# A 16-batch graph kernel: the first batch prepared in a fixed order, its adjacency loaded first on two queues, two layer norms in halves

## Chip, cores, metric

One core of a Trainium2 chip. The metric is the device time of one execution in microseconds (us), the median of several; the runs of any one kernel below lie within 0.24% of each other. A difference between two kernels counts as shown where the intervals of their ratios to the kernel before do not overlap; where they do, a trace must show it.

In the lines of profiles PE is TensorE, PEld its weight loads, DVE VectorE, ACT ScalarE, POOL GpSimd and SP the sync engine; a q behind a name is the part of an engine that issues DMAs. L12 is line 12 of the kernel that was run. One float32 matmul stands there as two records (x2): the 16 first products of a batch count as x32.

## What is computed

Two layers, each with a residual and a layer norm, over 16 graphs of 1024 nodes with 128 features. `adj` is 16 x 1024 x 1024 in float32, 4 MB a graph; `x` is 0.5 MB a graph.

```python
# layer 0
degree = adj.sum(axis=-1)[:, :, None]
agg = einsum('bid,bij->bjd', x, adj) / degree
x = layernorm(x + relu(concat([x, agg]) @ W.T + b))
# layer 1: four sublayers, the last two with the earlier features concatenated
def sub(nodes, ws, bs, wd, bd, wn, bn, wu, bu):
    src = einsum('bjv,bij->biv', nodes @ ws + bs, l2norm(adj, 2))   # rows scaled
    dst = einsum('bjv,bji->biv', nodes @ wd + bd, l2norm(adj, 1))   # columns scaled
    return tanh(concat([src, nodes @ wn + bn, dst]) @ wu + bu)
x = layernorm(x + sub(sub(...)))
```

## The kernel before

The four weights of a sublayer are folded once at the start: `ws`, `wd` and `wn` are each multiplied by their part of `wu`. The adjacency of a graph is then used in two forms: `a`, its columns scaled by `cinv`, and `at`, transposed, with its rows scaled by `rinv`. While TensorE multiplies one batch, the other engines prepare the next; only the first batch is prepared while TensorE has no matmuls of an earlier batch to run. This setup and first batch (the *head*) and the last norm (the *tail*) are what the change touches. Names that come up: `xn`, x with the nodes on the partitions; `pa`, the first products of x and the adjacency; `agT`, these divided by the degree; `pw`, their product with `W`; `pt` and `t`, the messages of a sublayer before and after their bias; `pd`, the aggregation of messages.

```python
with tc.tile_pool(name="setup", bufs=1) as sp:       # memory that later pools reuse
    make_identity(nc, ident)                          # GpSimd
    ...                                               # fold, mean, group: VectorE
    nc.scalar.dma_start(w0n, w0)
    for l, (ws, bs, wd, bd, wn, bn, wu, bu) in enumerate(layers):
        ...                                           # 8 loads a layer on ScalarE's queue
    for l, (wr, wur, bc) in enumerate(raw):           # folding: TensorE, copies on VectorE
        ...
        nc.vector.tensor_add(bo, pm[:, 2 * P:2 * P + 1], bc[:, 3:4])   # L139: bout

def load(b):                                          # all on one queue
    for h in range(NH):                               # two halves of the rows
        for g in range(G):                            # 4 groups of 32 partitions
            nc.sync.dma_start(a[g * C:(g + 1) * C, ks], av[g])
        for g in range(G):
            nc.sync.dma_start(xn[g * C:(g + 1) * C, ks], xv[g])   # L164
    ...

def sums(b, a, state, rows):
    for i in rows:
        nc.vector.reduce_sum(...)                     # degree
        nc.scalar.activation(sq, a[:, i, :], AF.Square, accum_out=...)
        nc.gpsimd.tensor_add(acc, acc, sq)            # L187, column sums, one after the other

# the first batch, in an order left to the scheduler
xn, xs, a = load(0)
sums(0, a, st, ALL); column_sums(0, st); inverses(0, st)
(cinv, dinv), rinv = inverse_rows(0, st, False)       # through a DRAM scratch
yT = first_gnn(0, xn, to_features(xs, "x0_", False), a, dinv)
ys, s = norm_begin(xs, yT, "0_0")
scale_columns(a, cinv, FIRST)
v = norm_centre(xs, ys, s, "0_0")
...
with tc.manual_schedule(engines={eng.PE, eng.DVE, eng.Activation}):
    for b in range(B):
        ...                                           # batch b, and batch b+1 prepared beside it
    ys, s = norm_begin(xs, f4, f"1_{B - 1}")          # the last norm, all 1024 nodes at once
    v = norm_centre(xs, ys, s, f"1_{B - 1}")
    rstd = norm_rstd(v, f"1_{B - 1}")                 # GpSimd power on 128x32
    norm_end(xs, rstd)
    store(B - 1, xs)
```

Of the kernel before, what the change touches and what calls it, by code (L numbers as in the profile page):

```python
# [23 lines left out]
def adj_resnorm_kernel(ctx: ExitStack, tc: tile.TileContext, x, adj, w0, b0, layers, out):  # L24
# [50 lines left out]

    fold = const.tile([P, P], F32, name="fold")
# [3 lines left out]
    nc.vector.memset(mhalf, -0.5)  # L80

    w0T = const.tile([P, 2, P], F32, name="w0T")
    b0c = const.tile([P, 1], F32, name="b0c")
    wall, bsd, bout = [], [], []

    with tc.tile_pool(name="setup", bufs=1) as sp:
        ident = sp.tile([P, P], F32, name="ident")
        make_identity(nc, ident)
        nc.vector.reduce_sum(fold[:, :C], ident.rearrange("p (g c) -> p c g", g=G), axis=AX.X)
        for g in range(1, G):  # L90
            nc.vector.tensor_copy(fold[:, g * C:(g + 1) * C], fold[:, :C])
        nc.vector.tensor_scalar_mul(mean, fold, 1.0 / D)
        nc.vector.reduce_sum(group, ident.rearrange("p (g c) -> p g c", g=G), axis=AX.X)
        w0n = sp.tile([P, 2 * P], F32, name="w0n")
        nc.scalar.dma_start(w0n, w0)
        nc.scalar.dma_start(b0c, b0.rearrange("(p o) -> p o", o=1))
        raw = []
        for l, (ws, bs, wd, bd, wn, bn, wu, bu) in enumerate(layers):
            nch = CHUNKS[l]
            wr = sp.tile([P, 3, nch, P], F32, name=f"wr{l}")  # L100
            for k, w in enumerate((ws, wd, wn)):
                nc.scalar.dma_start(wr[:, k], w.rearrange("(c p) v -> p c v", p=P))
            wur = sp.tile([P, 3, P], F32, name=f"wu{l}")
            nc.scalar.dma_start(wur, wu.rearrange("(c p) v -> p c v", p=P))
            bc = sp.tile([P, 4], F32, name=f"bc{l}")
            for k, v in enumerate((bs, bd, bn, bu)):
                nc.scalar.dma_start(bc[:, k:k + 1], v.rearrange("(p o) -> p o", o=1))
            raw.append((wr, wur, bc))

        pt = ps_t.tile([P, BPH, P], F32, tag="pt", name="w0tr")  # L110
        for k in range(2):
            nc.tensor.transpose(pt[:, k], w0n[:, k * P:(k + 1) * P], ident)
        nc.vector.tensor_copy(w0T, pt[:, :2])


        part = (0, 2, 1)
        for l, (wr, wur, bc) in enumerate(raw):
            nch = CHUNKS[l]
            wt = const.tile([P, nch, 3, P], F32, name=f"wall{l}")
            for c in range(nch):  # L120
                pt = ps_t.tile([P, BPH, P], F32, tag="pt", name=f"wtr{l}_{c}")
                for k in range(3):
                    nc.tensor.transpose(pt[:, k], wr[:, k, c], ident)
                wT = sp.tile([P, 3, P], F32, name=f"wT{l}_{c}", tag="wT", bufs=2)
                nc.vector.tensor_copy(wT, pt[:, :3])
                pm = ps_mm.tile([P, HW], F32, tag="mm", name=f"wm{l}_{c}")
                for k in range(3):
                    nc.tensor.matmul(pm[:, k * P:(k + 1) * P], wT[:, k], wur[:, part[k]],
                                     start=True, stop=True)
                nc.vector.tensor_copy(wt[:, c].rearrange("p k v -> p (k v)"), pm[:, :3 * P])  # L130
            pm = ps_mm.tile([P, HW], F32, tag="mm", name=f"bm{l}")
            for k in range(2):
                nc.tensor.matmul(pm[:, k * P:(k + 1) * P], bc[:, k:k + 1].to_broadcast([P, P]),
                                 wur[:, part[k]], start=True, stop=True)
            nc.tensor.matmul(pm[:, 2 * P:2 * P + 1], wur[:, part[2]], bc[:, 2:3], start=True, stop=True)
            bb = const.tile([P, 2 * P], F32, name=f"bsd{l}")
            nc.vector.tensor_copy(bb, pm[:, :2 * P])
            bo = const.tile([P, 1], F32, name=f"bout{l}")
            nc.vector.tensor_add(bo, pm[:, 2 * P:2 * P + 1], bc[:, 3:4])  # L139
            wall.append(wt)  # L140
            bsd.append(bb)
            bout.append(bo)
# [3 lines left out]
    stage = ctx.enter_context(tc.tile_pool(name="stage", bufs=3))  # L146

# [21 lines left out]
    def store(b, xs):  # L169
        ov = out[b].rearrange("(k r) (g f) -> g r k f", r=C, g=G)  # L170
        for g in range(G):
            nc.sync.dma_start(ov[g], xs[g * C:(g + 1) * C])

    def sums(b, a, state, rows):

        if not state:
            state["cols"] = two.tile([P, 3 * NB], F32, tag="cols", name=f"cols{b}")
            state["acc"] = one.tile([P, N], F32, tag="acc", name=f"acc{b}")
        cols, acc = state["cols"], state["acc"]
        for i in rows:  # L180
            nc.vector.reduce_sum(cols[:, 2 * NB + i:2 * NB + i + 1], a[:, i, :], axis=AX.X)  # L181
            sq = two.tile([P, N], F32, tag="sq", name=f"sq{b}_{i}")
            nc.scalar.activation(sq, a[:, i, :], AF.Square, accum_out=cols[:, i:i + 1])  # L183
            if i == 1:
                nc.gpsimd.tensor_add(acc, state["sq"], sq)
            elif i > 1:
                nc.gpsimd.tensor_add(acc, acc, sq)  # L187
            state["sq"] = sq
# [8 lines left out]

    def inverses(b, state):
# [10 lines left out]
        inv = two.tile([P, C], F32, tag="inv", name=f"inv{b}")  # L209
        nc.gpsimd.memset(inv[:, 3 * NB:], 0.0)  # L210
        nc.gpsimd.tensor_tensor(inv[:, :2 * NB], cols[:, :2 * NB], mhalf[:, :2 * NB], ALU.pow)
        state["inv"] = inv

    def inverse_rows(b, state, scaled):


        cols, inv = state["cols"], state["inv"]
        if scaled:
            nc.vector.tensor_mul(cols[:, 2 * NB:], cols[:, 2 * NB:], inv[:, NB:2 * NB])
        nc.vector.reciprocal(inv[:, 2 * NB:3 * NB], cols[:, 2 * NB:])  # L220
        tr = two.tile([P, C], F32, tag="invt", name=f"invt{b}")
        nc.vector.transpose(tr, inv)
        dr = scratch.tile([P, C], F32, tag="dr", name=f"dr{b}")
        nc.sync.dma_start(dr, tr)
# [7 lines left out]
        nc.vector.tensor_copy(rinv, pr)  # L232
        rows = []
# [7 lines left out]
        return rows, rinv  # L241

    def scale_columns(a, cinv, rows):
        for i in rows:
            nc.vector.tensor_mul(a[:, i, :], a[:, i, :], cinv)  # L245
# [12 lines left out]
    def norm_begin(xs, fT, name):  # L258
        ys = one.tile([P, K, C], F32, tag="acc", name=f"y{name}")
        nc.vector.transpose(ys.rearrange("p k f -> p (k f)"), fT)  # L260
        nc.vector.tensor_add(ys, ys, xs)
        s = two.tile([P, K], F32, tag="part", name=f"s{name}")
        nc.vector.reduce_sum(s, ys, axis=AX.X)
        return ys, s

    def norm_centre(xs, ys, s, name):
        pm = small(f"pm{name}")
        nc.tensor.matmul(pm, mean, s, start=True, stop=True)
        nc.vector.tensor_sub(xs, ys, pm[:, :, None].to_broadcast([P, K, C]))
        sq = two.tile([P, K, C], F32, tag="sq", name=f"sq{name}")  # L270
        nc.scalar.activation(sq, xs, AF.Square)
        v = two.tile([P, K], F32, tag="part", name=f"v{name}")
# [3 lines left out]
    def norm_rstd(v, name):  # L276
        pv = small(f"pv{name}")
        nc.tensor.matmul(pv, mean, v, start=True, stop=True)  # L278
        ve = two.tile([P, K], F32, tag="ve", name=f"ve{name}")
        nc.vector.tensor_scalar_add(ve, pv, LN_EPS)  # L280
        rstd = two.tile([P, K], F32, tag="rstd", name=f"rs{name}")
        nc.gpsimd.tensor_tensor(rstd, ve, mhalf, ALU.pow)  # L282
        return rstd

    def norm_end(xs, rstd):
        nc.vector.tensor_mul(xs, xs, rstd[:, :, None].to_broadcast([P, K, C]))  # L286
# [79 lines left out]


    FIRST, LAST, ALL = range(BPH), range(BPH, NB), range(NB)
    xn, xs, a = load(0)
    st = {}  # L370
    sums(0, a, st, ALL)
    column_sums(0, st)
    inverses(0, st)
    (cinv, dinv), rinv = inverse_rows(0, st, False)
    yT = first_gnn(0, xn, to_features(xs, "x0_", False), a, dinv)
    ys, s = norm_begin(xs, yT, "0_0")
    scale_columns(a, cinv, FIRST)
    v = norm_centre(xs, ys, s, "0_0")
    scale_columns(a, cinv, LAST)
    at = transposed(0)  # L380
    rows = [load_rows(0, q) for q in range(3)]
    scale_rows(rows[0], 0, rinv)
    rstd = norm_rstd(v, "0_0")
    transpose_rows(rows[0], 0, at)
    norm_end(xs, rstd)
    x1T = to_features(xs, "x1_0_", True)
    rows.append(load_rows(0, 3))
    for q in range(1, NQ):
        scale_rows(rows[q], q, rinv)
        transpose_rows(rows[q], q, at)  # L390
# [3 lines left out]
    eng = mybir.EngineType  # L394
    late = None
    with tc.manual_schedule(engines={eng.PE, eng.DVE, eng.Activation}):
# [133 lines left out]
```

## Time and profile before

| | before |
|---|---|
| median of 3 runs | 2744.63 us (2743.38 to 2747.24) |
| span of the profiled run | 2742.0 us |
| head: start to the first aggregation matmul | 109.2 us |
| block: from there to the end of the last matmul | 2610.4 us |
| tail: from there to the end | 22.4 us |

The three parts are read off the timeline and add up to the span. TensorE's busy share of 97% therefore does not close the matter: the block is nearly all TensorE and stays, and the other 132 us are open to change. The profile lines are shown in the prediction below.

### The profile page before, as it was taken

The page shows a single profiled execution, that of the slowest core. Times are in us where ns is not written, and L with a number is a line of the kernel's source. Part 1 is how long each engine was busy: PE and PEld are TensorE (multiplying, and loading weights), DVE is VectorE, ACT ScalarE, POOL GpSimd, SP SyncE. Part 2 cuts the span into 40 slices and gives each one's busy share as a digit, 9 for nine tenths or more (in the row PEclk, how much of TensorE's full clock was granted, in tenths as well). Part 3 has the DMA queues.
Part 4 walks back from the last instruction along what each step waited for, and adds up shares of the span by engine and source line. Part 5 has one row for each costly group of instructions (what it writes and reads, how often), then busy time and mean ns, then how long its engine had stood idle before and what let it go on. Part 6 is the DMA issues. An engine that isn't in the chain of part 4 may idle for free.

```text
span 2742.0 us, 18638 instructions
## 1 busy us (share of the span) xinstructions
PE 2661.1 (97%) x7257; PEld 1365.0 (50%) x7257; DVE 1150.7 (42%) x1581; ACT 286.9 (10%) x449; POOL 515.2 (19%) x182
## 2 busy tenths in 40 slices
PE   5699999999999999999999999999999999999996
PEld 3255554455545455554455545455554455545453
DVE  3634436253352634436253352634436253452501
ACT  1010101001010010101001010010101001010000
POOL 2021303113130121303113130121303113030100
PEclk8799999999999999999999999999999999999998
DMA  6811516134061431516134061431516134061100
GB/s 117 174 35 37 97 35 122 32 80 81 19 116 35 84 70 37 98 35 120 34 78 83 18 117 35 83 71 37 98 35 119 35 78 83 18 119 27 22 2 8
DMA packets 352504, 179.98 MB, mean 66 GB/s; under 512 B 151456, under 2 KB 336032, under 8 KB 352416
## 3 DMA queue, kind: packets, MB, share of 16 engines
q1 hardware_dynamic: 345344, 176.49, 33.0%
q10 hardware_dynamic: 7072, 2.30, 0.5%
q8 instruction: 57, 0.93, 0.2%
q14 instruction: 31, 0.25, 0.0%
HBM read 170.07 MB, written 8.65 MB: 65 GB/s over the span
## 4 chain that ended last, share of the span: by engine, by line
PE 96%; issue 1%; DMA 1%; POOL 1%; DVE 1%; POOLq 0%; ACTq 0%; SPq 0%; ACT 0%; DVEq 0%
PE pd L357 32%; PE pd L358 32%; PE pt L338 14%; PE pa L295 8%; PE pd L352 7%; PE pw L300 1%; PE pw L301 1%; DMA a<-in_adj_dram 0%; POOL acc L187 0%; DMA wu<-in_L_gnn_wu_dram 0%; DMA wr<-in_L_gnn_ws_dram 0%; POOLq L526 0%; POOL rs L282 0%; DMA w0n<-in_L_gnn_W_dram 0%; PE pv L278 0%
## 5 line engine op out<-in xcount | busy, mean ns | idle before, releaser
L357 PE MATMUL pd<-a,t 128*128 128x512 f32 x2048 | 1053.3, 596 | 0.0
L358 PE MATMUL pd<-at,t 128*128 128x512 f32 x2048 | 1045.8, 592 | 0.0
L358 PEld LDWEIGHTS pd<-at,t 128*128 128x128 f32 x2048 | 389.1, 190 | 489.8 <-issue 489.8
L357 PEld LDWEIGHTS pd<-a,t 128*128 128x128 f32 x2048 | 382.3, 190 | 446.8 <-issue 438.9
L282 POOL TENSOR_TENSOR rs<-ve,mhalf 128x32 f32<-128x32 f32 x32 | 202.6, 6330 | 1747.8 <-DVE ve L280 1747.8
L342 DVE TENSOR_TENSOR t<-pt,bsd 128x512 f32<-128x512 f32 x256 | 176.9, 691 | 491.9 <-PE pt L338 491.9
L295 PE MATMUL pa<-a,xn 128*128 128x512 f32 x512 | 229.2, 606 | 7.9 <-DMA xn<-in_x_dram 7.9
L187 POOL TENSOR_TENSOR acc<-acc,sq 128x1024 f32<-128x1024 f32 x96 | 226.0, 2354 | 34.0 <-ACT sq L183 27.8
L338 PE MATMUL pt<-wall,f1T 128*128 128x256 f32 x768 | 210.1, 379 | 0.0
L245 DVE TENSOR_TENSOR a<-a,cinv 128x1024 f32<-128x1024 f32 x128 | 146.9, 1219 | 112.7 <-DMA cinv<-dr 112.7
L296 DVE TENSOR_TENSOR agT<-pa,dinv 128x512 f32<-128x512 f32 x32 | 22.1, 692 | 388.6 <-PE pa L295 386.5
L321 DVE STREAM_TRANSPOSE at<-st 128x256 f32<-128x256 f32 x512 | 175.5, 407 | 10.2 <-PE pd L358 10.1
L295 PEld LDWEIGHTS pa<-a,xn 128*128 128x128 f32 x512 | 99.1, 194 | 132.1 <-issue 127.7
L338 PEld LDWEIGHTS pt<-wall,f1T 128*128 128x128 f32 x768 | 145.9, 190 | 33.5 <-issue 15.3
L181 DVE TENSOR_REDUCE cols<-a 128x1 f32<-128x1024 f32 x128 | 146.8, 1209 | 10.5 <-DMA a<-in_adj_dram 10.5
L183 ACT ACTIVATE sq<-a 128x1024 f32<-128x1024 f32 x128 | 134.5, 1052 | 134.9 <-POOL acc L187 82.0
L316 DVE TENSOR_TENSOR st<-st,rinv 128x2048 f32<-128x2048 f32 x64 | 145.7, 2276 | 2.0 <-DMA st<-in_adj_dram 1.6
L338 PE MATMUL pt<-wall,x_T 128*128 128x256 f32 x512 | 136.1, 384 | 7.8 <-DVE x_T L255 7.8
L338 PEld LDWEIGHTS pt<-wall,x_T 128*128 128x128 f32 x512 | 98.6, 193 | 34.9 <-issue 11.5
L352 PE MATMUL pd<-f1T,wall 128*128 128x512 f32 x192 | 98.0, 592 | 0.0
L286 DVE TENSOR_TENSOR xs<-xs,rs 128x1024 f32<-128x1024 f32 x32 | 39.2, 1226 | 132.1 <-POOL rs L282 132.1
L193 DVE STREAM_TRANSPOSE acct<-acc 128x1024 f32<-128x1024 f32 x16 | 19.9, 1246 | 174.3 <-POOL acc L187 174.3
(78 smaller groups left out, 1210.1 us busy)
## 6 DMA issues: line engine op xcount, KB each, us to landing
a<-in_adj_dram SPq DMA_DIRECT2D x128, 512.0 KB, 11.7
st<-in_adj_dram SPq DMA_DIRECT2D x512, 128.0 KB, 4.0
xn<-in_x_dram SPq DMA_DIRECT2D x128, 64.0 KB, 2.0
xs<-in_x_dram SPq DMA_DIRECT2D x64, 128.0 KB, 3.8
cinv<-dr SPq DMA_DIRECT2D x32, 256.0 KB, 5.4
dinv<-dr SPq DMA_DIRECT2D x32, 256.0 KB, 7.9
out_dram<-xs SPq DMA_DIRECT2D x64, 128.0 KB, 3.2
wu<-in_L_gnn_wu_dram ACTq DMA_DIRECT2D x4, 192.0 KB, 4.7
```

What stands on the lines that cost most here:

```text
L181: nc.vector.reduce_sum(cols[:, 2 * NB + i:2 * NB + i + 1], a[:, i, :], axis=AX.X)
L187: nc.gpsimd.tensor_add(acc, acc, sq)
L245: nc.vector.tensor_mul(a[:, i, :], a[:, i, :], cinv)
L282: nc.gpsimd.tensor_tensor(rstd, ve, mhalf, ALU.pow)
L295: nc.tensor.matmul(pa, xn[:, i], a[:, i, s], start=(i == 0), stop=(i == NB - 1))
L316: nc.vector.tensor_mul(st, st, rinv[:, q * QB:(q + 1) * QB, None].to_broadcast([P, QB, NH * P]))
L321: nc.vector.transpose(at[h][j][:, o:o + QB * C].rearrange("p (k c) -> p k c", c=C), st[:, :, j * C:(j + 1) * C])
L338: nc.tensor.matmul(pt[:, q], f[:, i * P:(i + 1) * P], w[:, c, 0:2].rearrange("p k v -> p (k v)"), start=(k == 0), stop=(k == nch - 1))
L342: nc.vector.tensor_add(d, pt, bsd[l][:, None, :].to_broadcast([P, 2, 2 * P]))
L352: nc.tensor.matmul(nodes(pd), w[:, c, 2], blocks(f[:, s]), start=(k == 0), stop=False)
L357: nc.tensor.matmul(pd, tj[:, P:], a[:, j, s], start=False, stop=False)
L358: nc.tensor.matmul(pd, tj[:, :P], at[h][j], start=False, stop=(j == NB - 1))
```

## The change

The intent: bring the adjacency of the first batch in first, on two queues; prepare the batch in an order fixed by hand on TensorE, VectorE and ScalarE; fold the weights in the gaps; avoid the scratch in DRAM for the first batch's factors; cut the first and the last norm into two halves, so that the last one's first half lies under the last matmuls.

```diff
-    with tc.tile_pool(name="setup", bufs=1) as sp:
-        ...                              # weights loaded and folded before all else
+    class Raw:                           # weights now lie in the second adjacency buffer
+        def __init__(self):
+            self.buf = apool.tile([P, NB, N], F32, tag="a", name="raw")...
+    def fetch_weights(raw, l): ...       # loads on the sync queue, after the adjacency
+    def fold_weights(l, fetched): ...    # the same products, copies on ScalarE
+    def factor_rows_now(b, k, inv, tag): # 8 transposes and 2 copies in place of the DRAM round trip
...
-    xn, xs, a = load(0)
+    for h in range(NH):
+        for k in range(0, BPH, 2):
+            for g in range(G):
+                q = nc.sync if g < G // 2 else nc.gpsimd
+                q.dma_start(a[g * C:(g + 1) * C, ks], av[g, :, k:k + 2])
+        for g in range(G):
+            nc.sync.dma_start(xn[...], xv[g])
+    ...                                  # xs, b0
+    fetched = [fetch_weights(raw, l) for l in range(NL)]
+    make_identity(nc, ident)             # after GpSimd's eight loads
...
+    for i in ALL:                        # squares, sums and first products as rows come
+        nc.scalar.activation(sq[i], a[:, i, :], AF.Square, accum_out=...)
+        nc.vector.reduce_sum(...)
+        ...                              # adds: half on GpSimd, half on VectorE
+        for h in range(NH):
+            nc.tensor.matmul(pa[h], xn[:, i], a[:, i, half(h)], ...)
...
+    fold_weights(0, fetched[0])
+    rows = [load_rows(0, q) for q in range(3)]
+    v = [norm_centre(xs, ys, s[h], KH[h], ...) for h in range(NH)]
+    fold_weights(1, fetched[1])
+    r = [norm_rstd(v[h], KH[h], ...) for h in range(NH)]
+    scale_columns(a, cinv, ALL, half(0))
+    for l in range(2, NL): fold_weights(l, fetched[l])
+    ...
+    for q in range(3):
+        scale_rows_now(rows[q], q)       # ScalarE instead of VectorE
+        if q < 2: transpose_rows(rows[q], q, at)
+    rows.append(load_rows(0, 3)); scale_rows_now(rows[3], 3)
+    late = [2, 3]                        # transposed after the t adds of batch 0
...                                      # in the loop, at the last batch only:
+            w["s"] = norm_begin(xs, w["ys"], f4, KH[0], ...)
+            h1 = {2: centre_last, 5: rstd_last}      # hooks among the last matmuls
-    ys, s = norm_begin(xs, f4, f"1_{B - 1}")
-    ...
+    norm_end(xs, w["r"], KH[0]); store(B - 1, xs, KH[0])
+    s = norm_begin(xs, w["ys"], f4, KH[1], ...)
+    ...                                  # second half likewise
```

## The prediction

Measured in before: 216 and 202 GB/s with only 32-partition loads under way; 16 message matmuls in 5.73 us after TensorE had been mostly idle (1.3 us busy from 85 to 100 us, granted clock 0.50) and in 3.45 us at clock 1.00; one add of 128x1024 in 2.35 us on GpSimd and 1.21 on VectorE. The eight slots are in the trace of before too: up to 75 us no more than eight loads are under way at a time; eight are issued from 0.73 to 3.59 us, and the ninth at 6.01, after the first two had landed (5.78 and 5.99). pw, which the prediction has waiting for agT, waited 3.4 us for it there.

Three terms of the sum are each an estimate with no trace behind its number: a rate above 215 GB/s, which gave the early end of "17 to 23 us" for the rows; the time of a GpSimd load, which put the identity at about 10 us, from where VectorE's 24.7 is counted; and the loss of a cold start before the first aggregation, which makes T+54 out of the 52.4.

> **What bounds the kernel now.** I read the page first, then the busy time by stretches, then the chain of work and the timeline of the first 140 us and of the last 25. In the stretches, the columns after the second number are the busy time and count of each engine, then the granted clock, the DMA share and GB/s.
>
> ```profile
> PE 2661.1 (97%) x7257; PEld 1365.0 (50%) x7257; DVE 1150.7 (42%) x1581; ACT 286.9 (10%) x449; POOL 515.2 (19%) x182
> ...
> 300.00:1000.00 700.00, 700.00 (x1916) 359.60 (x1915) 300.21 (x407) 82.32 (x131) 149.06 (x52) 1.00 0.35 68
> 1000.00:2700.00 1700.00, 1700.00 (x4631) 869.85 (x4630) 702.98 (x961) 171.00 (x266) 302.50 (x100) 1.00 0.31 61
> ```
>
> TensorE is busy for all of these two stretches at full clock, and the waits between 110 and 2719 us list none for it. So batches 1 to 15 are a fixed block of matmuls, and the change leaves their instructions and order alone (the comparison of instruction orders shows the same sequence from there on). Only the head, before the first aggregation matmul, and the tail, after the last, can move. The head ends in the timeline at 109.19 us, the first L357, already at full clock. Its chain:
>
> ```profile
> 34.27 11.59 DMA a<-in_adj_dram
> ...
> 47.25 2.37 POOL acc L187
> ...
> 60.93 2.93 POOL inv L211
> ...
> 95.27 5.44 POOL rs L282
> ...
> 102.76 5.73 PE pt L338 x16
> ```
>
> Adjacency rows are still arriving at 45.9 us; GpSimd then adds four squares in a row (to 56.9), raises to a power (2.93), raises again (5.44), and TensorE starts in earnest at 102.76. Why the rows are late:
>
> ```profile
> SPq L164 <- DVE bout L139: 2.2, 1, 2.2
> ```
>
> The load of xn on the sync queue waits for bout, the last result of the weight folding: xn lies in memory that the setup pool held. The second half of the adjacency is queued behind it, so it goes out only at 32.85 us, after 28 us in which the first half shared the queues' eight completion slots with 34 weight loads. The tail, from the timeline:
>
> ```profile
> 2719.58 0.69 ACT L362 ACTIVATE f4T<-pd,bout 128x512 f32<-128x512 f32 x1 [15.56 <-PE pd L358]
> 2720.30 1.25 DVE L260 STREAM_TRANSPOSE y<-f4T 128x1024 f32<-128x1024 f32 x1 [32.65 <-ACT f4T L362]
> ...
> 2729.19 5.43 POOL L282 TENSOR_TENSOR rs<-ve,mhalf 128x32 f32<-128x32 f32 x1 [129.43 <-DVE ve L280]
> ...
> 2735.90 2.67 SPq L172 DMA_DIRECT2D out_dram<-xs  x4
> ```
>
> A serial norm over all 1024 nodes with every other engine idle, 22.4 us from the last matmul to the end at 2742.0.
>
> [...] with only 32-partition loads under way it moved 216 and 202 GB/s from 35 to 45 us at a DMA share of 1.00 and 1.04. The change puts partitions 0 to 63 on one queue and 64 to 127 on the other[...]. [...] no run here shows two such streams yet. [...] 16 of L338 took 5.73 us at 102.76 and 3.45 at 137.68. [...] Here 2.35 against 1.21 us on 128x1024.
>
> **The change, part by part.** The repeated blocks of batches 1 to 15 cost nothing new. In the head:
>
> (a) Arrival. Nothing waits for the folding any more. Before the last rows come 4.2 MB of adjacency, 0.13 of W0 and 0.26 of xn, 4.6 MB. At the single-queue 215 GB/s that is 21 us, [...] with some 2 us to start, 17 to 23 us instead of 45.9.
>
> (b) What follows the rows as they come. GpSimd now issues eight loads before it builds the identity, and VectorE's setup and ScalarE's w0T copy, both first in fixed orders, wait for it. No trace here has a GpSimd load[...]. VectorE then has 1.2 us of setup, 8 sums of 1.21 and 3 adds of 1.22: 24.7. Counted from rows that land at T, the last add ends at T+4.9 (sum, add, sum, add), so this pace equals T=19.9. TensorE's 32 pa instructions are 13.8 us warm; begun at about 12 (xn lies behind half of the rows) with a cold start, they end at some 27, about T+8, level with VectorE. I take T=20.5.
>
> (c) From T to the first aggregation, with durations of before, halved where the shape is. VectorE: four steps to 4.9, reciprocal and acc to 6.3, transpose and sum to 8.7, x's transpose to 10.0, two agT at 0.69 to 11.4. TensorE's pw must wait for agT to free its bank: 4 cold instructions from 10.7 to 14.1, relu to 14.9, second half 17.0, transposes, adds and sums of the norm to 18.9; the power for inv (2.9) lies beside this. Row inverses (sp, TensorE, rinv, 1.0) 20.0. Now queued in order before the centring: eight transposes and two copies for cinv, 22.6, and fold 0, 2.7, 25.3. Centring, squares and sums of two halves, 29.2; fold 1 interleaved, pv and ve, 31; two powers of 2.9 (the 128x16 form), 36.5, with the column scaling (8 of 0.63) beside; ends and transposes of two halves, 39. Folds 2 and 3 run from 30.5: ScalarE has 2.9 and 4.0 us of copies (0.58, 0.46 and 0.2 us by shape, estimated from its 0.69 for 512 columns), and cold TensorE's turns between add some 4.5: 42. Only then does ScalarE scale the rows, 16 instructions of 128x256 at an estimated 0.44 (1.05 us for 1024 columns, 0.69 for 512) = 7: 49. Eight transposes of the second quarter, 2.7, and the first t add, 0.7, both ordered before the aggregation: 52.4. [...] About T+54, less 1.5 for overlaps I priced as serial: T+52.5.
>
> Sum: 20.5 + 52.5 = 73 against 109.2, **36 saved**. Of it 25 are earlier rows and 11 a shorter chain (63.3 before).
>
> (d) Tail. The first half's norm lies under the last 16 us of matmuls: its pieces are done by about 15.7 of them. What remains is the second half: tanh 0.7; transpose, add, sum, centre, v, end at 0.65 each; TensorE 0.4 and 0.65; square 0.6; ve 0.2; power 2.9; hops 0.3: 9.6, then half the store, 5.5 for 6.1. 15.1 against 22.4: **7 saved**, less 0.3 for two small matmuls put into the stream.
>
> 2744.6 - 36 - 6.7 = **2702 us**, 1.5% less.
>
> **The rivals.** Folded weights come late: 33 small transfers queue behind the adjacency, in the space of batch 1's adjacency, and centring stands behind fold 0 on TensorE. The eight slots at some 5 us a load (the page has 2.2 to 5.4) give 20 us, so the last weights at about 43 to 45, while fold 3 comes at 20.5+36=56. Against it: 11 us of slack. If they came at 65, the time would be 2711. Second rival: a stall moves into batch 0. Batch 1's adjacency may load only when fold 3 is over, and waits behind the fourth quarter of rows, so from about 70 to 97 us; its squares are wanted after the first layer, 29 us after the head's end, at 102. Narrow; 10 us lost would give 2712. Third: [...] all rows land by 15, the loads are issued faster than I think, and the ScalarE chain is shorter by 5: head 62, time 2690, on the border of 2%. [...] Against it: pace (b) does not depend on arrival. Fourth: GpSimd's loads are slow [...]: identity at 18, head 81, time 2710.
>
> **Range and chances.** The head may be 63 to 83, the tail's gain 5 to 8; together 2691 to 2712 for 8 in 10. More than 2% faster needs under 2689.7, a head of about 61, which takes the third rival in full: 0.08. Slower by 2% would need 55 us of new stalls against a TensorE stream that is unchanged: 0.01. Within 2%: 0.91.
>
> **What would show it.** The last adjacency rows land between 15 and 24 us, and the first aggregation matmul starts between 63 and 83, with ScalarE's scaling and VectorE's transposes of the second quarter the last thing before it. ScalarE, not GpSimd, is then what the head's chain runs over most. TensorE waits for nothing after it, the block up to its last matmul stays 2610 us, and the last matmul is followed by some 15 us with one power of 2.9. I am wrong if the rows still land after 30, if TensorE waits in batch 0 for batch 1's adjacency, or if the chain after the rows is under 45 or over 60.

## The result

| | before | after |
|---|---|---|
| median | 2745.03 us (2743.38 to 2747.24, 4 runs) | 2702.68 us (2702.11 to 2704.99, 4 runs) |
| ratio | | 0.9847 (0.983 to 0.9864) |
| profiled span | 2742.0 us | 2700.8 us |
| head | 109.2 us | 75.1 us |
| block | 2610.4 us | 2610.7 us |
| tail | 22.4 us | 15.0 us |

Ratios, here and below, are the mean time of one kernel's runs over that of the other's of the same rounds, so not quite the ratio of the medians quoted. The change saved 1.5%, which counts as the same within 2%; the intervals leave no doubt that it is faster.

The head of after is told as the moment from which TensorE runs the block at full speed: its first aggregation matmul is at 71.97, but the first four matmuls are slow, which costs 3.2 us. The parts: 34.1 us from the head, 7.4 from the tail, -0.3 from the block, 41.2 in all.

On the page of after TensorE is busy for 98% of the span. The busy time by stretches has the block (columns as in the prediction: window, length, then busy time and count of TensorE, its weight loads, VectorE, ScalarE, GpSimd, then the clock, the DMA share and GB/s):

```profile
300.00:1000.00 700.00, 700.00 (x1908) 358.04 (x1907) 297.67 (x405) 73.45 (x115) 129.72 (x45) 1.00 0.34 66
1000.00:2680.00 1680.00, 1680.00 (x4584) 861.08 (x4583) 695.53 (x952) 170.93 (x266) 304.31 (x99) 1.00 0.31 60
```

TensorE is busy in every microsecond of both stretches, as it was. So nothing given to the head was taken back later; the second rival would have shown as idle time in batch 0. Between 70 us and the last matmul the waits of TensorE have a single entry (engine, tile and line, what it waited for, total, count, longest):

```profile
PE pd L370 <- DVE t L355: 6.2, 1, 6.2
```

That is the wait before the very first aggregation matmul. The chain of work that ended last in after, with start, duration and instruction:

```profile
5.11 12.95 DMA a<-in_adj_dram
18.06 16.54 PE pa L441 x32
...
35.69 0.70 DVE agT L450
...
64.10 4.49 ACT st L478 x11
69.31 2.03 DVE at L334 x6
71.34 0.59 DVE t L355
71.97 2.07 PE pd L370 x2
74.05 1.71 PE pd L371 x2
75.75 1.71 PE pd L370 x2
77.46 1.11 PE pd L371 x2
78.57 0.86 PE pd L370 x2
```

Against the chain before, GpSimd's adds and powers are gone. It is now a wait for DMA until 18, TensorE's first products (16 matmuls, 32 records) until 34.6, a long chain of small steps, ScalarE's scaling of rows, VectorE's transposes and the t add. In before, the 30.9 us between the two powers stand in the chain as "issue", for which the profile names no releaser; in the timeline VectorE waits there 5.1 us for `cinv` and 2.1 us for `dinv`, which come back from DRAM at 71.4 and 75.3 us. What the round trip alone cost was not tested.

The last five lines show the cold start: a matmul takes 2.07, 1.71, 1.71 and 1.11 us before it takes 0.86. Four took 6.6 us where four at 0.86 take 3.4. The granted clock, the third number from the right, was 0.51 from 72 to 78 us, and 1.00 again from 79:

```profile
72.00:78.00 6.00, 6.00 (x8) 2.49 (x9) 4.34 (x11) 2.13 (x6) 0.00 (x0) 0.51 1.07 215
```

The timeline of after (start, busy time, engine, line, operation, tiles, count; in brackets the idle time before and what ended it) for the arrival:

```profile
1.31 4.37 POOL L399 DMA_DIRECT2D a<-in_adj_dram  x8 [0.86 <-POOLq L625]
3.07 2.00 SPq L401 DMA_DIRECT2D xn<-in_x_dram  x4
...
9.10 1.06 ACT L432 ACTIVATE sq<-a 128x1024 f32<-128x1024 f32 x1 [1.66 <-DMA a<-in_adj_dram]
...
18.06 16.54 PE L441 MATMUL pa<-a,xn 128*128 128x512 f32 x32 [11.02 <-DMA a<-in_adj_dram]
...
22.85 1.06 ACT L432 ACTIVATE sq<-a 128x1024 f32<-128x1024 f32 x1 [0.29 <-DMA a<-in_adj_dram]
```

Two things are to be seen. The last rows are in ScalarE's hands at 22.85, inside the predicted 17 to 23. And the first rows are there at 9.10, while the products that use them start at 18.06. The trace names the adjacency as what released them; that cannot be the whole of it, since ScalarE was squaring the same rows 9 us before. The other operand is xn, whose first four loads stand on the sync queue behind the first four loads of rows there (1 MB). In e8, a run of the same kernel, the trace names xn:

```profile
17.85 16.75 PE L441 MATMUL pa<-a,xn 128*128 128x512 f32 x32 [10.81 <-DMA xn<-in_x_dram]
```

Experiment e2 tests it, and the section on e4 shows why xn is so late.

The tail of after, in the same columns:

```profile
2683.82 0.69 DVE L296 TENSOR_TENSOR xs<-xs,rs 128x512 f32<-128x512 f32 x1 [3.08 <-POOL rs L291]
...
2684.76 1.02 PE L371 MATMUL pd<-at,t 128*128 128x512 f32 x2
2685.82 0.69 ACT L375 ACTIVATE f4T<-pd,bout 128x512 f32<-128x512 f32 x1 [9.27 <-PE pd L371]
...
2692.42 2.90 POOL L291 TENSOR_TENSOR rs<-ve,mhalf 128x16 f32<-128x16 f32 x1 [8.63 <-DVE ve L289]
```

The first half is finished (L296) before the last matmul ends. What follows it is one half, with a power of 2.90 us where before it took 5.43: 15.0 us to 2700.8.

### The profile page after: what moved, and what is told of

Same layout as the page of the kernel before. It is cut to its first block, busy times and chain, and to the rows that moved or that the text cites. A ratio compares the mean times of both kernels' runs of the same rounds, so it can differ in the third digit from the quotient of the medians.

```text
span 2700.8 us, 18782 instructions
## 1 busy us (share of the span) xinstructions
PE 2656.3 (98%) x7281; PEld 1364.1 (51%) x7281; DVE 1139.0 (42%) x1579; ACT 310.9 (12%) x510; POOL 512.9 (19%) x188
## 4 chain that ended last, share of the span: by engine, by line
PE 98%; DVE 1%; DMA 0%; ACT 0%; SPq 0%; POOLq 0%; issue 0%; ACTq 0%; DVEq 0%
PE pd L370 33%; PE pd L371 33%; PE pt L351 14%; PE pa L308 8%; PE pd L365 7%; PE pw L314 1%; PE pw L313 1%; PE pa L441 1%; DMA a<-in_adj_dram 0%; PE wm L136 0%; ACT st L478 0%; PE pv L287 0%; PE pm L276 0%; POOLq L635 0%; PE rp L224 0%
## 5 line engine op out<-in xcount | busy, mean ns | idle before, releaser
L370 PE MATMUL pd<-a,t 128*128 128x512 f32 x2048 | 1055.4, 597 | 6.2 <-DVE t L355 6.2
L371 PE MATMUL pd<-at,t 128*128 128x512 f32 x2048 | 1046.9, 593 | 0.0
L371 PEld LDWEIGHTS pd<-at,t 128*128 128x128 f32 x2048 | 389.7, 190 | 490.9 <-issue 490.9
L370 PEld LDWEIGHTS pd<-a,t 128*128 128x128 f32 x2048 | 382.5, 190 | 453.1 <-issue 438.9
L291 POOL TENSOR_TENSOR rs<-ve,mhalf 128x32 f32<-128x32 f32 (+1 forms) x34 | 205.5, 6044 | 1717.3 <-DVE ve L289 1717.3
L181 POOL TENSOR_TENSOR acc<-acc,sq 128x1024 f32<-128x1024 f32 x90 | 211.9, 2354 | 24.8 <-ACT sq L177 18.9
L308 PE MATMUL pa<-a,xn 128*128 128x512 f32 x480 | 208.4, 592 | 0.0
L251 DVE TENSOR_TENSOR a<-a,cinv 128x1024 f32<-128x1024 f32 (+1 forms) x136 | 147.4, 1154 | 110.1 <-DMA cinv<-dr 110.1
L308 PEld LDWEIGHTS pa<-a,xn 128*128 128x128 f32 x480 | 91.2, 190 | 114.8 <-issue 114.8
L177 ACT ACTIVATE sq<-a 128x1024 f32<-128x1024 f32 x120 | 126.1, 1052 | 116.3 <-POOL acc L181 79.2
L175 DVE TENSOR_REDUCE cols<-a 128x1 f32<-128x1024 f32 x120 | 137.7, 1209 | 0.0
L329 DVE TENSOR_TENSOR st<-st,rinv 128x2048 f32<-128x2048 f32 x60 | 136.6, 2276 | 0.1
L351 PEld LDWEIGHTS pt<-wall,x_T 128*128 128x128 f32 x512 | 97.2, 190 | 26.4 <-issue 11.5
L279 ACT ACTIVATE sq<-xs 128x1024 f32<-128x1024 f32 (+1 forms) x34 | 34.2, 1006 | 524.2 <-DVE xs L277 524.2
L296 DVE TENSOR_TENSOR xs<-xs,rs 128x1024 f32<-128x1024 f32 (+1 forms) x34 | 39.5, 1161 | 129.4 <-POOL rs L291 129.4
```

Source lines behind the costliest of these rows:

```text
L175: nc.vector.reduce_sum(cols[:, 2 * NB + i:2 * NB + i + 1], a[:, i, :], axis=AX.X)
L251: nc.vector.tensor_mul(a[:, i, s], a[:, i, s], cinv[:, s])
L291: nc.gpsimd.tensor_tensor(rstd, ve, mhalf[:, :n], ALU.pow)
L308: nc.tensor.matmul(pa, xn[:, i], a[:, i, s], start=(i == 0), stop=(i == NB - 1))
L329: nc.vector.tensor_mul(st, st, rinv[:, q * QB:(q + 1) * QB, None].to_broadcast([P, QB, NH * P]))
L351: nc.tensor.matmul(pt[:, q], f[:, i * P:(i + 1) * P], w[:, c, 0:2].rearrange("p k v -> p (k v)"), start=(k == 0), stop=(k == nch - 1))
```

## The experiments

Each run was beside runs of the kernel before on the same chip; all results were correct. They are ordered by question, not by time; e5 and e10 to e12 ran on another chip than the rest. The medians of before were 2746.01 us (7 runs) beside e1 to e4, 2745.44 (8 runs) beside e6 to e9 and 2746.74 (9 runs) beside e5 and e10 to e12. Some texts of what was expected call the changed kernel after.

### The tail alone: e1 and e10

e1 undoes the last norm's halves in after; e10 does them alone in the kernel before.

```diff
 # e1, on after
-        else:
-            w = {"ys": summed(f"y1_{b}")}
-            ...                                     # first half under the last matmuls
-    norm_end(xs, w["r"], KH[0])
-    ...
+    ys = summed(f"y1_{B - 1}")
+    s = norm_begin(xs, ys, f4, KS, f"1_{B - 1}")
+    v = norm_centre(xs, ys, s, KS, f"1_{B - 1}")
+    r = norm_rstd(v, KS, f"1_{B - 1}")
+    norm_end(xs, r, KS)
+    store(B - 1, xs, KS)
 # e10, on before: the same lines the other way round, and helpers of the norm that take a range of nodes
```

> The changed kernel with the last layer norm whole again, as before. Main theory: the tail part is worth what the two profiles show, 22.4 us against 15.0 from the last matmul to the end, less some 0.3 us for two small matmuls, so this run takes 7 us more: 2709 to 2711 us, with one power of 5.4 us after the last matmul and the head unchanged (first L370-like aggregation at 72 us). Rival: the store or the queue drain sets the end, then under 3 us more.

> The kernel before with only the last layer norm in halves. Theory (head and tail are independent ends of an unchanged block): ratio to before 0.9973, that is 7 us less, 2738 us, the same 7 us that undoing it costs the changed kernel. Rival (they interact): under 4 or over 10 us.

e1: 2709.8 us (2708.06 to 2711.99), ratio 0.9868 (0.9852 to 0.9885), 7.1 us over after. e10: 2736.86 us (2735.12 to 2741.46), ratio 0.9968 (0.9955 to 0.9982), which is 8.8 us under before, with an interval of 5 to 12. The interval of e1 overlaps a little with that of after, and that of e10 leaves room for the rival's 10 us, so the traces decide: from the last matmul to the end e1 takes 22.9 us and e10 14.8, where before took 22.4 and after 15.0. The timeline of e1 has the whole power back:

```profile
2695.41 5.43 POOL L291 TENSOR_TENSOR rs<-ve,mhalf 128x32 f32<-128x32 f32 x1 [129.65 <-DVE ve L289]
```

So the tail's part is 7.4 to 7.9 us in the traces, with the old head and with the new one: the term of 7 in the prediction is shown.

### The second queue and its partitions: e2 and e3

```diff
-                q = nc.sync if g < G // 2 else nc.gpsimd
+                q = nc.sync                                        # e2
+                q = nc.sync if g % 2 == 0 else nc.gpsimd           # e3
```

> The changed kernel with all adjacency loads of batch 0 on the sync queue. Theory A (what holds TensorE at 18.06 us is xn, last in line behind a queue that gets half of the transfer rate; one queue of 32-partition loads moves 205 to 215 GB/s): xn's first half lands at about 14 us, the last rows at about 24, TensorE's pa ends at 32 to 33 in place of 34.6, agT starts at 34 to 35 in place of 35.7, time 2700 to 2703 us: the second queue gains nothing. Theory B (the second queue brings the rows earlier and that is a main part of the gain): rows 4 us or more later, time 2706 us or more.

> The changed kernel with partition groups 0 and 2 on the sync queue and 1 and 3 on the GpSimd queue[...]. [...] 205 to 215 GB/s between 5 and 15 us in place of 233 to 255, rows and xn 1.5 to 3 us later, time 2704 to 2706 us. Rival (the rate comes from having two queues[...]): 233 to 255 GB/s as before, time within 1 us of 2702.7.

e2: 2699.21 us (2698.31 to 2701.6), ratio 0.9831 (0.9816 to 0.9846). e3: 2702.34 us (2700.58 to 2703.99), ratio 0.9841 (0.9826 to 0.9856). The stretches from 5 to 15 us, of after, then e2, then the first of e3 (its second has 241); the last number is GB/s:

```profile
5.00:10.00 5.00, 0.69 (x2) 0.29 (x2) 2.04 (x7) 1.27 (x2) 1.28 (x6) 1.00 1.04 255
10.00:15.00 5.00, 0.00 (x0) 0.00 (x0) 3.80 (x4) 3.48 (x8) 3.55 (x2) 1.00 1.08 233
```

```profile
5.00:10.00 5.00, 0.00 (x0) 0.00 (x0) 1.54 (x2) 1.55 (x3) 0.00 (x0) 1.00 1.06 219
10.00:15.00 5.00, 0.32 (x1) 0.35 (x2) 2.56 (x3) 2.40 (x5) 2.80 (x2) 1.00 1.09 213
```

```profile
5.00:10.00 5.00, 0.69 (x2) 0.29 (x2) 1.61 (x7) 0.83 (x2) 1.30 (x6) 1.00 1.05 263
```

Two queues move 9 to 16% more than one in these stretches. e3, with the groups dealt out the other way, is not slower than after. e3 was to have both queues load the same half of the partitions at a time, to see whether the gain needs different halves. But e3 does not do what it was meant to do: the queues would have to run in step. Up to 9 us its sync queue had moved 1.12 MB (0.13 of it W0) and GpSimd's 0.67, which is more than one load of 0.26 MB ahead, so much of the time the two stood on different halves. Whether the rate of two queues has to do with the partitions that they load stays open.

And the higher rate buys nothing. The timeline of e2:

```profile
14.68 9.12 PE L441 MATMUL pa<-a,xn 128*128 128x512 f32 x16 [11.02 <-DMA xn<-in_x_dram]
...
33.94 1.29 DVE L450 TENSOR_TENSOR agT<-pa,dinv 128x512 f32<-128x512 f32 x2
```

With one queue the last rows come 1.5 us later (24.31), but the first products start 3.4 us sooner, now with xn named as their release, and agT starts 1.75 us sooner. Giving xn's queue the whole adjacency moved the rows later and the products earlier, so it was xn that held them in after. The median is 3.5 us under that of after, 0.8 below the range that was expected, but the intervals of the ratios overlap, and the profiles don't decide: the second half of the nodes starts at 87.90 us, against 88.71 in after and 86.32 in e8. It is not settled that one queue is faster, only that no gain from the second is seen.

### xn ahead of the rows: e4

```diff
+    for h in range(NH):
+        for g in range(G):
+            nc.sync.dma_start(xn[...], xv[g])       # both halves first
     for h in range(NH):
         for k in range(0, BPH, 2):
             ...                                     # rows as in after, two queues
-        for g in range(G):
-            nc.sync.dma_start(xn[...], xv[g])
```

> The changed kernel with both halves of xn loaded ahead of the adjacency. Theory A (TensorE's pa, begun late for xn's sake, sets the start of agT): pa starts at 9 to 11 us, its last matmul ends within 5 us of the last rows (27 to 29), agT starts when VectorE gets there, at 33 to 34 in place of 35.7, time 2700 to 2701 us. Rival (VectorE's order or the dinv copies set it anyway): agT stays at 35 to 36, time 2702 to 2703 us.

2707.2 us (2704.25 to 2708.09), ratio 0.9857 (0.9842 to 0.9872). Neither theory had a slower kernel. The interval overlaps with that of after; the trace has the first aggregation matmul at 76.58 us, 4.6 later. Of e4, the first DMA of the chain, then the first square in the timeline:

```profile
3.56 8.80 DMA xn<-in_x_dram
```

```profile
18.92 1.06 ACT L433 ACTIVATE sq<-a 128x1024 f32<-128x1024 f32 x1 [11.45 <-DMA a<-in_adj_dram]
```

The DMA of the chain is the sixth of xn's eight loads: although first on their queue, it landed only at 12.36 us. Up to then the sync queue had moved 0.60 MB of 2.29, 26%, and GpSimd's, with rows, the rest. The first rows came at 18.9 instead of 9.1, as the sync queue's part of them waited behind xn; VectorE's sums then ran to 34 and agT started at 38.97, 3.3 us later than in after.

xn comes in 512-byte pieces, the rows in 4 KB pieces (in after, from 9 to 15 us, 333 packets have 512 bytes to 2 KB and 306 more), and the queue with the small pieces got the smaller part. The trace of after shows the same. Its GpSimd queue (q0) and sync queue (q1), with packets, MB and the time of the packets as a share of 16 engines, from 5 to 9 us, with rows on both:

```profile
q1 hardware_dynamic: 175, 0.53, 54.7%
q0 software_dynamic: 149, 0.49, 49.3%
```

From 9 to 15 us, when the sync queue comes to xn:

```profile
q0 software_dynamic: 382, 1.25, 91.0%
q1 hardware_dynamic: 375, 0.18, 16.4%
```

With pieces of one size the two queues shared the bytes evenly (0.53 and 0.49 MB); with xn against rows they moved as many packets each (375 and 382), and the sync queue a seventh of the bytes. So it is the small pieces beside the other queue that made xn late, and moving xn forward doesn't help while that queue is running. By what rule the queues share is not shown: in e4, from 5 to 9 us, the sync queue moved 358 packets to GpSimd's 212, and still only 0.16 MB to 0.70.

### The adjacency first: e5

```diff
     nc.sync.dma_start(w0n, w0)
+    raw = Raw()
+    fetched = [fetch_weights(raw, l) for l in range(NL)]
     ...                                             # rows, xn, xs
-    raw = Raw()
-    fetched = [fetch_weights(raw, l) for l in range(NL)]
```

> The changed kernel with its weight loads ahead of the adjacency on the sync queue. Theory (adjacency first is needed: 2.2 MB and 33 transfers go ahead of half of the rows): last rows at 30 to 34 us in place of 22.9, agT at 42 to 46 in place of 35.7, time 2709 to 2713 us. Rival (it was the waiting for the folding that held the rows back in the kernel before, and the order of loads matters little): within 2 us of 2702.7.

2717.34 us (2715.39 to 2719.38), ratio 0.9895 (0.9881 to 0.9908), 14.7 us over after and 4 more than the worst that was expected. By the ratios, which allow for the other chip, it is 13 to 14. The timeline of e5:

```profile
32.62 16.91 PE L441 MATMUL pa<-a,xn 128*128 128x512 f32 x32 [28.98 <-DMA xn<-in_x_dram]
```

The weights ran to about 25 us, and the first products started 14.6 us later than in after, almost exactly the time lost. So the order of loads, undone in after, is worth about 15 of the head's 34 us. The other 19 (xn no longer waiting for the folding's memory, and the shorter chain after the rows) were not taken apart.

### Halves in the first norm: e7, and after once more: e8

```diff
-        s.append(norm_begin(xs, ys, yT, KH[h], f"0_0_{h}"))
+    s = norm_begin(xs, ys, yT, KS, "0_0")
     ...
-    v = [norm_centre(xs, ys, s[h], KH[h], f"0_0_{h}") for h in range(NH)]
+    v = norm_centre(xs, ys, s, KS, "0_0")
-    r = [norm_rstd(v[h], KH[h], f"0_0_{h}") for h in range(NH)]
+    r = norm_rstd(v, KS, "0_0")
     ...                                             # norm_end likewise
```

> The changed kernel with the first layer norm of batch 0 whole again. Theory (halves hide nothing in the head, where the two halves run one after the other on the same engines: start of the norm whole 1.1 us later at the sums, centring 0.6 shorter, power 5.4 for 5.9, ends equal): first aggregation within 1 us of 72, time within 1 us of the changed kernel. Rival (halves in the head are worth what they are in the tail, several us): 3 us or more longer.

> The changed kernel as it is, on the chip of the next three runs, for a direct comparison. Any theory: 2702 to 2704 us; first aggregation matmul at 72 us.

e8, after unchanged: 2702.86 us (2700.42 to 2703.15), ratio 0.9843 (0.983 to 0.9857). e7: 2703.34 us (2703.15 to 2703.48), ratio 0.9845 (0.983 to 0.9859). The halves of the first norm gain nothing that can be seen: the medians are 0.5 us apart, less than the runs of e8 spread, against 7 for those of the last one. In the last norm the first half had a place under matmuls; in the first one, the trace of after has its two powers of 2.9 from 53.50 to 59.43 us, one right after the other, while the folding of the weights ends only at 61.96: one whole power of 5.4 fits in the same place. In the chain of e8 the first aggregation matmul starts at 70.37: 1.6 us sooner than in the first profile of the same kernel, and the second half of its nodes 2.4 us sooner. Differences of this size between two profiles mean nothing; they limit what e2 and the next runs can say.

### Scaling on VectorE again: e11

```diff
-        scale_rows_now(rows[q], q)                  # ScalarE, 8 instructions of 128x256
         if q < 2:
+            scale_rows(rows[q], q, rinv)            # VectorE, one of 128x2048
             transpose_rows(rows[q], q, at)
+        else:
+            scale_rows_now(rows[q], q)
```

> The changed kernel with the first two quarters of rows scaled on VectorE, 2.27 us each, as before, in place of ScalarE's 16 instructions. Theory (ScalarE's 6.6 us come after its folding; VectorE is free from 61.2 and would be done with both quarters by 61.2+2.3+2.7+2.3+2.7 = 71.2, where it is now at 71.3): within 1 us of the changed kernel, so moving the scaling to ScalarE gained nothing in the head. Rival (ScalarE's scaling is the change's gain in this part): 2 us or more longer.

2701.89 us (2700.93 to 2702.17), ratio 0.9838 (0.9824 to 0.9851), the same as after within its interval. Its first aggregation matmul is at 71.28, and the timeline of e11 has the scaling on VectorE:

```profile
60.70 2.25 DVE L329 TENSOR_TENSOR st<-st,rinv 128x2048 f32<-128x2048 f32 x1
```

The scaling of rows moved to ScalarE saves nothing in the head. On ScalarE it starts when the folding's copies end and VectorE waits for it; on VectorE it adds 2.25 us a quarter to VectorE's own row of work. One is as long as the other.

### t before the transposes: e6, e9 and e12

The last two steps before the first aggregation are transposes and t adds, both on VectorE, in a fixed order with the transposes first. But the first of the two matmuls for each block of nodes (L370) needs only t and `a`; the second (L371) needs the transposes. These runs put the t adds first, so that only the second waits.

```diff
 # e6; e9 is e6 with q = nc.sync; e12 is e9 with the last two hunks
     for q in range(3):
         scale_rows_now(rows[q], q)
-        if q < 2:
-            transpose_rows(rows[q], q, at)
-    rows.append(load_rows(0, 3))
-    scale_rows_now(rows[3], 3)
-    late = [2, 3]
+    late = [0, 1, 2, 3]
 ...
         for q in late:                              # after messages(), the t adds
             transpose_rows(rows[q], q, at)
+            if b == 0 and q == 0:
+                rows.append(load_rows(0, 3))
+                scale_rows_now(rows[3], 3)
 # e12 only
-        if nxt:
+        if nxt and b > 0:
             xn2, xs2, a2 = load(n)
 ...
         if b == 0:
+            xn2, xs2, a2 = load(n)                  # after the fourth quarter's load
```

> The changed kernel with batch 0's four t additions ahead of the transposes of the first two quarters on VectorE (and the fourth quarter's load after the first transposes). Theory (VectorE idles 4.2 us for ScalarE's scaling while pt lies ready, so the 2.45 us of additions fit there, and TensorE can start after the first transposes of the second quarter, which wait for the scaling at 68.6): first aggregation matmul at 69 to 69.5 us in place of 71.97, time about 2.5 to 3 us less than the changed kernel, 2699.5 to 2700.5. Rival (pt or something else on TensorE sets the start, or the later load of the fourth quarter stalls the second half): no gain or a loss.

> All adjacency of batch 0 on the sync queue, and the t additions first. If both gains are real and lie on the same chain one after the other, 0.5 to 1.5 us from the queue and 2.5 to 3 from the order: 2698 to 2700 us, the fastest so far. If the one-queue run was faster by chance only (its head was but 0.5 us shorter in the profile), it equals the run with the t additions alone within 0.5 us.

e6: 2717.67 us (2716.65 to 2718.67), ratio 0.9897 (0.9882 to 0.9912). e9: 2715.83 us (2714.75 to 2718.56), ratio 0.9893 (0.9877 to 0.991). Both are 13 to 15 us slower than after and some 17 slower than their theories had it; the rival of e6 had named what happened, a stall by the later load of the fourth quarter. The fault was in the edit. In after the load of the fourth quarter of rows is issued before the loop, and so before the 5 MB of batch 1. The edit moved it behind them on the same queue. Of e6, the waits, then the timeline:

```profile
PE pd L370 <- DVE a L251: 18.3, 1, 18.3
```

```profile
95.53 3.29 ACT L478 ACTIVATE st<-st,rinv 128x256 f32<-128x256 f32 x8 [24.64 <-DMA st<-in_adj_dram]
```

TensorE's first half did begin early, at 65.12, but then waited 18.3 us in front of the second half. The trace names the scaled `a` of VectorE; VectorE works in a fixed order and stood behind the fourth quarter's transposes, which stood behind ScalarE, which had waited 24.64 us for the load.

> One queue and the t additions first, with batch 1's load now queued behind the fourth quarter of batch 0's rows (in the two runs before, it had got in front, and the second half of the first layer waited 18.3 us for that quarter by way of VectorE). Theory: TensorE's first half starts as early as there (its first matmul of the second half came 5.8 us before the changed kernel's) and nothing waits later; with 1 to 2.5 us of the one queue: 2695 to 2698 us, the fastest. Rival (the start gained is lost again, as VectorE or batch 1's rows then come late): 2700 us or more.

e12, with the loads in their old order: 2694.21 us (2693.52 to 2696.79), ratio 0.9812 (0.9799 to 0.9825), whose interval lies below that of after (0.983 to 0.9857 in e8, 0.983 to 0.9864 at first) and has the 2% mark within it. It beats both kernels, by about 52 us and by 8.5. The timeline of e12:

```profile
63.97 1.02 PE L370 MATMUL pd<-a,t 128*128 128x512 f32 x2
...
67.49 1.12 PE L371 MATMUL pd<-at,t 128*128 128x512 f32 x2 [2.50 <-DVE at L334]
...
80.47 1.02 PE L365 MATMUL pd<-x_T,wall 128*128 128x512 f32 x2
```

The same place in after, the start of the second half of the nodes:

```profile
88.71 1.02 PE L365 MATMUL pd<-x_T,wall 128*128 128x512 f32 x2
```

The first matmul comes 8.0 us sooner and without a wait before it, and it is warm: it takes 1.02 us, and the one after the wait of 2.5 us takes 1.12, where in the timeline of after the first takes 2.07. So the 3.2 us of cold start are not paid; the 2.5 us are given back to the wait for the transposes. 8.0 + 3.2 - 2.5 = 8.7, and 88.71 - 80.47 = 8.2 is what the second half shows (5.9 against the profile of e8). Most of it is the order: in e6, whose stall comes only after this point, the second half starts at 82.91, and with one queue besides it starts at 80.77 (e9) and 80.47 (e12). The last 2 us, which would be the single queue's, are within what two profiles of one kernel differ by.

## Why the prediction was right

The time (2702.68 for 2702) and the mechanism were right: a fixed block, a head cut by the arrival of rows and a shorter chain, a tail cut by half a norm. Not all of its steps were, and that the time came out to the microsecond is luck: two misses cancelled. Its split of the head, 25 us of earlier rows and 11 of a shorter chain, came out at 23.1 and 11.0. Step by step, predicted against the profile of after:

| step | predicted | measured |
|---|---|---|
| identity built | about 10 us | 6.3 |
| last rows land | 20.5 | 22.8 |
| first products start, end | 12, 27 | 18.06, 34.60 |
| agT starts | 30.5 | 35.69 |
| agT to the end of the folds | 32.0 | 26.3 |
| scaling of 16 rows on ScalarE | 7.0 | 6.5 |
| last transposes and first t add, end | 72.9 | 71.93 |
| loss of the cold start | | 3.2 |
| head | 73 | 75.1 |
| tail | 15.1 | 15.0 |

- **Arrival and first products.** The rows came within the range predicted, at 255 and 233 GB/s; the higher rate that its early end rested on was not seen. That xn "lies behind half of the rows" was seen, but was priced as a start at 12 us. It was 18.06: while xn was loading, from 9 to 15 us, its queue moved 0.18 MB and the other one 1.25. This made TensorE, not VectorE, the last one before agT: VectorE waited 2.3 us for it. The rest of agT's 5.2 us is VectorE's own, which got its last rows 2.3 us later than the 20.5 taken. e2 confirms the cause: with one queue the products start at 14.68, and VectorE doesn't wait before agT.
- **From agT to the end of the folds.** 5.7 us less than worked out. The first products ran until 34.60, so TensorE was warm when pw came (granted clock 1.00 from 36 to 40 us): pw took 2.0 us and not the 3.4 that the prediction has for cold ones. ScalarE's copies, estimated from a larger shape, were 0.48 us for 384 columns (0.58 estimated) and 0.37 for 256 (0.46), and folds 2 and 3 took 8.7 us (53.28 to 61.96) in place of 11.5. The first miss may have caused a part of this gain, as the late products kept TensorE busy until just before pw; no run tests that.
- **Scaling and the last VectorE steps** were right in order and size: the chain shows ScalarE's scaling, then the transposes, then t, then the matmul. They were taken as given, though, when the t adds could go first, which is where e12 finds its gain.
- **The cold start** was priced at about half of what it cost, by an estimate that no trace gave: four slow matmuls, 3.2 us, with the granted clock at 0.51 for some 6 us (72 to 78). In the nine profiles with this wait it was 2.4 to 3.2 us; the trace that the prediction quotes had 2.3 already (5.73 less 3.45).
- **"ScalarE, not GpSimd"**, as what the chain runs over most, is half right. GpSimd is gone from it, but its longest parts are TensorE's: 16.5 us of first products and some 11 of folding, with ScalarE's scaling at 5.8.
- **The tail** was right to 0.1 us, and e1 and e10 show it apart from the rest.
- **Two slips of sums** in (b) changed nothing: 10 + 1.2 + 8 x 1.21 + 3 x 1.22 is 24.5 and not 24.7, and an end of the products at 27 is T+6.5 and not T+8.

Of the rivals, late weights and a stall in batch 0 are refuted by TensorE's waits: none for the load of a weight before 72 us and none at all after it, with batch 1's squares from 104.09 not holding it. The third, that all rows land by 15 us, is refuted by the rows (22.8) and the rate (255 and 233 GB/s). Slow loads on GpSimd are refuted by the timeline: eight took 4.37 us to issue, 0.55 each.

Two parts of the change earn nothing that these runs can see: the second queue (e2) and the halves of the first norm (e7). Moving the scaling to ScalarE doesn't either (e11).

## What to carry to other kernels

When one engine is busy for the whole middle of a kernel, price the head and the tail alone, and check afterwards that the middle kept its length. In a head, order the loads by who needs them first, look for the operand that comes last rather than the largest, and do first on each engine what the first instruction of the bound engine needs. When an instruction moves, look at which queue its load moves to the end of: in e6 a load behind 5 MB of another batch cost far more than the reordering gained.
